# The inputs' part of an LSTM's gates: formed for eight steps at a time and turned by the identity, with the gates in three PSUM banks

## The chip, the core and the metric

The kernel runs on one core of a Trainium2 chip. The metric is the device time of one execution in microseconds; the time given is the median of several executions. The profile is one further execution, recorded by the hardware profiler; its span runs from the first to the last instruction on the core. Its engines are PE (matrix multiplication), DVE (vector), ACT (activation functions), POOL (general purpose) and SP (which here only issues DMA transfers).

## The reference

The inputs are `x`, 32 sequences of 512 rows with 256 features, and an adjacency matrix for each sequence. Two layers follow one another, each a graph attention and a sequence model, each with a layernorm ahead of it and the input added to what it gives. The last of the four parts is an LSTM with something behind it, and the change is about that:

```python
x_proj = jnp.einsum('btd,gd->btg', x, W_ih) + b_ih + b_hh
def step(carry, xp):
    h, c = carry
    gates = xp + h @ W_hh.T
    i, f, g, o = jnp.split(gates, 4, axis=-1)
    c = jax.nn.sigmoid(f) * c + jax.nn.sigmoid(i) * jnp.tanh(g)
    h = jax.nn.sigmoid(o) * jnp.tanh(c)
    return ((h, c), h)
...
logits = jnp.einsum('bth,lh->btl', lstm_out, W_lin) + b_lin
g = jax.lax.stop_gradient(jnp.argmax(logits, axis=-1)...)[..., None]
w = g * lstm_out
inc = jnp.cumsum(w, axis=1)
prefix = inc - w
suffix = inc[:, -1:, :] - inc
return 2.0 * lstm_out + prefix * fw_att + suffix * bw_att
```

Here B = 32 sequences, T = 512 steps, H = 256 hidden units, so 1024 gate values for each sequence and step. A step needs h of the step before: the 512 steps are a chain. The argmax over two logits is a comparison of their difference with a level. Everything is float32.

## The kernel before

The program has two stages. `layers_per_batch` does the first three parts sequence by sequence and leaves the result in DRAM as `X3`, with time outermost. `recurrence` then does the LSTM for all 32 sequences at once. Between the two stands a branch that is taken only for unusual data.

**Layout of a step.** The 256 hidden units are cut into Q = 4 groups of J = 64. Partition 32 q + b holds sequence b and group q, so the 128 partitions are full, and a gate of all sequences is 64 columns wide. The products therefore have 32 sequences as the stationary operand and run as four column tiles of 32 in PE, one for each q, each into its 32 partitions of PSUM. The launch code lays the gates down as i, f, o, g; `order` in `recurrence_weights` takes them as 1, 0, 3, 2, so a step has blocks of 64 columns for f, i, g and o, and two more columns for the difference of the logits and a zero. The sigmoid of v is taken as (tanh(v/2) + 1)/2, with the halves folded into the weights, so one tanh serves all gates. W = 258.

**A step in its parts.** PSUM has two tiles for a step, `pga` with 192 columns (f, i, g) and `pgb` with 66 (o, logit).
- `opened` (line 1201) starts each with the bias: a product of `one`, a row of ones in partition 0, with `bg`, which holds the biases in partition 0 and zeros elsewhere.
- `add_to` (line 1208) adds the inputs' part: the transposed input `xTr` of this step against `wih`, and later h against `whh`. Each is K = 256 deep, hence two products for each q.
- ACT takes the tanh of `pga` (line 1267) and of the o part of `pgb` (line 1268), into `z`, whose first 64 columns hold the cell.
- DVE forms `ab` (line 1270), (f+1)·c and (i+1)·g in one instruction over 128 columns, the new cell (line 1276), ACT its tanh `tc` (line 1278), DVE h as `hh` (line 1281) and its transpose within blocks of 32 (line 1283), which is what the next product needs.
- DVE then compares the logit that came with this step's product, which belongs to the step before (line 1289), and adds to the running sum `pp` (line 1293).

**Order.** The recurrence is written with the order of PE, DVE and ACT by hand: instructions stand in each engine's queue as the loop emits them. PE gets h's part of step t and then bias and inputs' part of step t+1, and in some steps the transposes of coming inputs. DVE gets behind the step one piece of `extra`: work for the chunk before or after. A chunk is CH = 16 steps. `normalised` loads four tiles `xt` of the next chunk (128 rows, 4 steps each), takes their statistics in steps 0 to 3, normalises them, and transposes them on PE in steps 11 to 14 (line 1142), ACT copying from PSUM (line 1145). `results` adds up the output of the chunk before in ten pieces (lines 1167 to 1179) and sends it to `R`, which stays in SBUF until the total over all steps is known; the last lines add that and write the output. DMA issues on SP are placed by the framework's scheduler.

**Weights.** `recurrence_weights` scales and reorders the weights on POOL during the layers and writes them to a DRAM tensor `wr`, and the biases to `wrb`; `recurrence` loads them with three DMAs from ACT (lines 1100 to 1102).

Of the kernel before, what the change touches and what calls it, by code (L numbers as in the profile page):

```python
# [19 lines left out]
P = 128  # L20
# [55 lines left out]
def layers_per_batch(ctx, tc, c, a, X3, odd=None, wr=None):  # L76
# [898 lines left out]
    if odd is not None:  # L975
        rw = ctx.enter_context(tc.tile_pool(name="rw0", bufs=1))
        parts = 2 + 2 + 2 * DK * 4
        streams.append(4.25 + nb / 2 * n / parts for n, _ in enumerate(recurrence_weights(nc, rw, a, wr)))
# [33 lines left out]
def recurrence_weights(nc, pool, a, wr):  # L1012
# [3 lines left out]

    Q, J = 4, 64
    W = 4 * J + 2
    nw = DK * Q * W
    order = ((1, 0.5), (0, 0.5), (3, 1.0), (2, 0.5))  # L1020
# [4 lines left out]
    def ordered(raw, n, s):  # L1025
        t = tile_(P, W, "rwt")
        nc.gpsimd.memset(t[:n, 4 * J :], 0.0)
        for to, (g, f) in enumerate(order):
            nc.gpsimd.tensor_scalar(t[:n, to * J : (to + 1) * J], raw[:n, g * J : (g + 1) * J], f * s, None, ALU.mult)
        return t  # L1030
# [3 lines left out]
    for q in range(Q):  # L1034
        for l in range(2):
            nc.sync.dma_start(
                out=wl[q * 32 : (q + 1) * 32, l * DK : (l + 1) * DK],
                in_=a.wl[q : q + 1, l * J : (l + 1) * J].rearrange("o (k p) -> p (o k)", p=32),
            )
    nc.gpsimd.tensor_tensor(wl[:, :DK], wl[:, DK:], wl[:, :DK], ALU.subtract)  # L1040
    yield
    bl = tile_(Q, 2, "rbl")
    nc.sync.dma_start(out=bl, in_=a.bl.to_broadcast([Q, 2]))
    b = [tile_(P, 4 * J, f"rwraw{n}") for n in range(2)]
    for t, src in zip(b, (a.bih, a.bhh)):
        nc.sync.dma_start(out=t[:Q], in_=src.rearrange("o (q r) -> (o q) r", q=Q))
    nc.gpsimd.tensor_tensor(b[0][:Q], b[0][:Q], b[1][:Q], ALU.add)
    t = ordered(b[0], Q, 1.0)
    nc.gpsimd.tensor_tensor(t[:Q, 4 * J : 4 * J + 1], bl[:, 1:2], bl[:, 0:1], ALU.subtract)
    nc.sync.dma_start(out=wr[1].rearrange("o (q w) -> (o q) w", q=Q), in_=t[:Q])  # L1050
    yield
    for n, src in enumerate((a.fw, a.bw)):
        t = tile_(P, W, "rwt")
        for q in range(Q):
            nc.sync.dma_start(out=t[q * GB : (q + 1) * GB, :J], in_=src[q : q + 1, :].to_broadcast([GB, J]))
        nc.gpsimd.tensor_scalar(t[:, :J], t[:, :J], 0.5, None, ALU.mult)
        nc.sync.dma_start(out=wr[0][:, 2 * nw + n * J : 2 * nw + (n + 1) * J], in_=t[:, :J])
        yield
    for n, (src, s) in enumerate(((a.wih, 1.0), (a.whh, 0.5))):
        for k in range(DK):  # L1060
            for q in range(Q):
# [8 lines left out]
                t = ordered(raw, P, s)  # L1070
                if n == 1:
                    nc.gpsimd.tensor_scalar(t[:, 4 * J : 4 * J + 1], wl[:, k : k + 1], 0.5, None, ALU.mult)
                o0 = n * nw + (k * Q + q) * W
                nc.sync.dma_start(out=wr[0][:, o0 : o0 + W], in_=t)
# [3 lines left out]
def recurrence(ctx, tc, c, a, X3, wr, out):  # L1078
# [6 lines left out]
    WA, WB = 3 * J, J + 2  # L1085
    W = WA + WB
# [5 lines left out]
    psg = ctx.enter_context(tc.tile_pool(name="psg", bufs=3, space=PSUM))  # L1092
    psx = ctx.enter_context(tc.tile_pool(name="psx", bufs=2, space=PSUM))


    wall = wp.tile([P, 2 * DK * Q * W + 2 * J], F32, name="wall")
    bg = wp.tile([P, Q, W], F32, name="bg")
    nc.gpsimd.memset(bg, 0.0)
    nw = DK * Q * W
    nc.scalar.dma_start(out=wall[:, :nw], in_=wr[0][:, :nw])  # L1100
    nc.scalar.dma_start(out=bg[0:1].rearrange("o q w -> o (q w)"), in_=wr[1])
    nc.scalar.dma_start(out=wall[:, nw:], in_=wr[0][:, nw:])
    wih, whh = (wall[:, n * nw : (n + 1) * nw].rearrange("p (k q w) -> p k q w", k=DK, q=Q) for n in range(2))
    fw, bw = (wall[:, 2 * nw + n * J : 2 * nw + (n + 1) * J] for n in range(2))
    one = wp.tile([P, GB], F32, name="one")
    nc.vector.memset(one, 0.0)
    nc.vector.memset(one[0:1, :], 1.0)
# [8 lines left out]
    def normalised(t0, out_):  # L1116
# [4 lines left out]
        for n in range(NX):  # L1121
            xt = xp_.tile([P, D], F32, tag=f"xt{n}", name=f"xt{t0}_{n}")
# [15 lines left out]
        def turn(n):  # L1138
# [4 lines left out]
            xT = xp_.tile([P, DK, P], F32, tag=f"xT{n}", name=f"xTr{t0}_{n}")  # L1143
            out_[n] = xT
# [4 lines left out]
    def results(t0, hh, gh, pp):  # L1149
# [9 lines left out]
        for s in (slice(0, n), slice(n, CH)):  # L1159
# [3 lines left out]
            m = gh[:, s, :]  # L1163
# [30 lines left out]
    PARTS = ((0, WA, "pga"), (WA, W, "pgb"))  # L1194

    def opened(t):

        pg = [psg.tile([P, e - s], F32, tag=tag, name=f"{tag}{t}") for s, e, tag in PARTS]
        for (s, e, _), p in zip(PARTS, pg):
            for q in range(Q):  # L1200
                nc.tensor.matmul(p[q * GB : (q + 1) * GB, :], one, bg[:, q, s:e], start=True, stop=False)  # L1201
        return pg

    def add_to(pg, x, w, stop):
        for (s, e, _), p in zip(PARTS, pg):
            for k in range(DK):
                for q in range(Q):
                    nc.tensor.matmul(  # L1208
                        p[q * GB : (q + 1) * GB, :], x[:, k, :], w[:, k, q, s:e],
                        start=False, stop=(stop and k == DK - 1),  # L1210
                    )

    def x_part(t, xT):

        pg = opened(t)
        r = (t % 4) * GB
        add_to(pg, xT[:, :, r : r + GB], wih, t == 0)
        return pg

    def blocks(z, n):  # L1220

        return bass.AP(tensor=z.tensor, offset=z.offset, ap=[list(z.ap[0]), [n * J, 2], [1, J]])

    with tc.manual_schedule(engines={mybir.EngineType.PE, mybir.EngineType.DVE, mybir.EngineType.Activation}):
        xT = [None] * NX
        stats, norms, turns = normalised(0, xT)
# [4 lines left out]
        nxt = [None] * NX  # L1231
        extra, turning = [], {}
        pg = x_part(0, xT[0])
# [4 lines left out]
        h = hh = gh = None  # L1238
        for t in range(T + 1):
            s = t % CH  # L1240
            last = t == T
            if s == 0 and not last:
                t0 = t
                hh_was, gh_was, pp_was = hh, gh, pp
                hh = ch.tile([P, CH, J], F32, tag="hh", name=f"hh{t0}")
                gh = ch.tile([P, CH, J], F32, tag="gh", name=f"gh{t0}")
                if t:
                    xT, nxt = nxt, [None] * NX
                    pp = ch.tile([P, CH + 1, J], F32, tag="pp", name=f"pp{t0}")
                assert not extra and not turning  # L1250
                stats, norms, turns = normalised(t0 + CH, nxt) if t0 + CH < T else ([], [], [])
                more = results(t0 - CH, hh_was, gh_was, pp_was) if t else []
                both = [lambda fs=norms[n : n + 2]: [f() for f in fs] for n in range(0, len(norms), 2)]
                extra = stats + more[:3] + both[:1] + more[3:4] + both[1:] + more[4:]
                turning = {CH - NX - 1 + n: f for n, f in enumerate(turns)}
            if last:

                pg = opened("last")
            if t:
                add_to(pg, h, whh, True)  # L1260
            pga, pgb = pg
            if not last:
                if t + 1 < T:
                    pg = x_part(t + 1, (xT if s + 1 < CH else nxt)[(s + 1) % CH // 4])
                turned = turning.pop(s)() if s in turning else None

                nc.scalar.activation(z[:, J : 4 * J], pga, AF.Tanh)  # L1267
                nc.scalar.activation(z[:, 4 * J :], pgb[:, :J], AF.Tanh)
                ab = st.tile([P, 2 * J], F32, tag="ab", name=f"ab{t}")
                nc.vector.scalar_tensor_tensor(  # L1270
                    ab.rearrange("p (a b) -> p a b", a=2), z[:, J : 3 * J].rearrange("p (a b) -> p a b", a=2),
                    1.0, blocks(z, 3), ALU.add, ALU.mult,
# [6 lines left out]
                if turned:  # L1279
                    turned()  # L1280
# [4 lines left out]
            if t:  # L1285

                i = (t - 1) % CH
                g_, p_, h_ = (gh_was, pp_was, hh_was) if s == 0 and not last else (gh, pp, hh)
                nc.vector.scalar_tensor_tensor(
                    g_[:, i, :], pgb[:, J : J + 1].to_broadcast([P, J]), 0.0, h_[:, i, :],  # L1290
# [122 lines left out]
```

## Time and profile before

| | before |
|---|---|
| median of 3 executions | 5133.64 us (5131.93 to 5137.21) |
| profiled execution, time | 5135.78 us |
| its span | 5134.1 us |
| layers, up to the first instruction of the recurrence | 3599 us |
| first tanh of a step to the last | 3613.0 to 5066.5 us |
| PE, DVE, ACT, POOL busy over the span | 83%, 64%, 55%, 21% |
| PE's granted clock, mean over the span | 0.936 |
| PE's granted clock, 500 to 3500 us, and 3700 to 5000 us | 0.93 to 0.94, and 1.00 |

Of the profile's views, four are used. The chain that ended last goes back from the last instruction to what released each one, and gives the shares of the span that lie on it by engine and line. The groups join instructions of the same line and tiles, with their number and mean duration in ns. The timeline gives instructions in order of time, neighbours of a kind merged, with their start and duration in us. The page of a line or tile gives durations as min/median/max and the times of the first and last one. In the last two, `128*32` is the size of the part of PE that an instruction uses and `x16` the number merged; a float32 product is two instructions. A PE duration includes the way through the array, so neighbours overlap; where one group follows another without a break, the time from start to start is what counts.

### The profile page before, as it was taken

The page shows a single profiled execution, that of the slowest core. Times are in us where ns is not written, and L with a number is a line of the kernel's source. Part 1 is how long each engine was busy: PE and PEld are TensorE (multiplying, and loading weights), DVE is VectorE, ACT ScalarE, POOL GpSimd, SP SyncE. Part 2 cuts the span into 40 slices and gives each one's busy share as a digit, 9 for nine tenths or more (in the row PEclk, how much of TensorE's full clock was granted, in tenths as well). Part 3 has the DMA queues.
Part 4 walks back from the last instruction along what each step waited for, and adds up shares of the span by engine and source line. Part 5 has one row for each costly group of instructions (what it writes and reads, how often), then busy time and mean ns, then how long its engine had stood idle before and what let it go on. Part 6 is the DMA issues. An engine that isn't in the chain of part 4 may idle for free. (4 is left out here: it accounts for less than half of the span.)

```text
span 5134.1 us, 129165 instructions
## 1 busy us (share of the span) xinstructions
PE 4260.7 (83%) x55022; PEld 2706.9 (53%) x55022; DVE 3279.2 (64%) x8158; ACT 2824.2 (55%) x5770; POOL 1096.5 (21%) x917
## 2 busy tenths in 40 slices
PE   4788888888888888888888888887788888888884
PEld 2344455444444445544445444454667666767663
DVE  3566666666666666666666666664566666666666
ACT  3677666776667766677666777664222222222221
POOL 4223232223332233322333223321000000000000
PEclk7899899999999999999999999998999999999997
DMA  3111112211122111211112121111211111111114
GB/s 107 56 60 54 56 55 69 65 50 60 50 66 66 56 58 52 66 63 60 58 52 66 58 64 58 52 42 33 61 41 34 37 39 41 41 37 37 38 36 150
DMA packets 272285, 288.48 MB, mean 56 GB/s; under 512 B 151509, under 2 KB 223025, under 8 KB 269522
## 3 DMA queue, kind: packets, MB, share of 16 engines
q1 hardware_dynamic: 268032, 268.09, 17.3%
q10 hardware_dynamic: 3506, 11.99, 0.7%
q8 instruction: 433, 7.09, 0.6%
q14 instruction: 154, 1.26, 0.1%
q0 software_dynamic: 160, 0.04, 0.0%
HBM read 226.04 MB, written 37.11 MB: 51 GB/s over the span
## 5 line engine op out<-in xcount | busy, mean ns | idle before, releaser
L1208 PE MATMUL pga<-wall,h 128*32 128x192 f32 x8176 | 438.3, 332 | 175.3 <-DVE h L1283 168.1
L1267 ACT ACTIVATE z<-pga 128x192 f32<-128x192 f32 x512 | 169.2, 330 | 691.8 <-PE pga L1208 684.5
L777 ACT ACTIVATE g<-bc,cs 128x128 f32<-128x128 f32 x1024 | 325.8, 390 | 341.1 <-PE py L803 334.8
L1208 PE MATMUL pga<-wall,xTr 128*32 128x192 f32 x8192 | 428.7, 326 | 0.0
L693 DVE SCALAR_TENSOR_TENSOR acc<-px,convw,acc 128x509 f32<-128x509 f32 (+2 forms) x480 | 341.6, 742 | 96.4 <-ACT acc L688 94.3
L533 PE MATMUL pav<-w,hb 128*64 128x512 f32 x1024 | 352.9, 617 | 60.2 <-DVE w L467 60.2
L461 ACT ACTIVATE w<-rb,neg,colsa 128x512 f32<-128x512 f32 x512 | 388.8, 804 | 8.0 <-DMA rb<-linea 4.3
L729 POOL TENSOR_TENSOR xdd<-xdt,dec 128x512 f32<-128x512 f32 x96 | 98.9, 1043 | 1348.9 <-DVE xdt L712 1348.4
L937 PE MATMUL pov<-wb,wv 128*128 128x257 f32 x1024 | 288.6, 450 | 106.7 <-DVE bnmv L66 94.9
L1208 PEld LDWEIGHTS pga<-wall,h 128*32 128x32 f32 x8176 | 213.6, 109 | 301.9 <-DVE h L1283 268.7
L803 PE MATMUL py<-g,xdt 128*64 128x128 f32 x2048 | 172.6, 320 | 225.9 <-DVE g L782 209.9
L467 DVE SCALAR_TENSOR_TENSOR w<-w,adjT 128x1024 f32<-128x1024 f32 x256 | 308.6, 1218 | 31.1 <-ACT w L461 31.1
L937 PEld LDWEIGHTS pov<-wb,wv 128*128 128x128 f32 x1024 | 232.8, 231 | 156.5 <-issue 113.0
L672 PE MATMUL px<-mT,win 128*128 128x512 f32 x640 | 300.6, 609 | 0.0
L54 POOL TENSOR_SCALAR ve<-mv 128x4 f32<-128x4 f32 x32 | 6.2, 193 | 1349.9 <-DVE mv L1129 1349.9
L1270 DVE SCALAR_TENSOR_TENSOR ab<-z 128x128 f32<-128x128 f32 x512 | 149.8, 293 | 224.0 <-ACT z L1267 224.0
L1278 ACT ACTIVATE tc<-z 128x64 f32<-128x64 f32 x512 | 131.4, 257 | 288.7 <-DVE z L1276 288.7
L790 POOL TENSOR_TENSOR xh<-xh,zs 128x512 f32<-128x512 f32 x128 | 179.6, 1404 | 512.1 <-DVE wb L926 348.5
L803 PEld LDWEIGHTS py<-g,xdt 128*64 128x64 f32 x2048 | 134.5, 160 | 280.8 <-DVE g L782 237.7
L822 PE MATMUL po<-wc,xh 128*128 128x256 f32 x1024 | 242.4, 391 | 27.6 <-POOL xh L790 27.4
L1201 PE MATMUL pga<-bg,one 128*32 128x192 f32 x4096 | 261.1, 326 | 0.0
L56 POOL TENSOR_TENSOR rs<-ve,mhalf 128x4 f32<-128x4 f32 (+1 forms) x192 | 255.0, 1328 | 16.0
(259 smaller groups left out, 9873.0 us busy)
## 6 DMA issues: line engine op xcount, KB each, us to landing
bc<-line SPq DMA_DIRECT2D x128, 512.0 KB
adj<-in_adj_dram SPq DMA_DIRECT2D x32, 1024.0 KB
rb<-linea SPq DMA_DIRECT2D x64, 512.0 KB
ce<-line SPq DMA_DIRECT2D x64, 384.0 KB
x<-in_x_dram SPq DMA_DIRECT2D x32, 512.0 KB
X<-x SPq DMA_DIRECT2D x32, 512.0 KB
xt<-X SPq DMA_DIRECT2D x128, 128.0 KB
x<-X SPq DMA_DIRECT2D x128, 128.0 KB
```

The lines of the kernel that those rows point to most:

```text
L56: nc.gpsimd.tensor_tensor(rs, ve, c.mhalf[:, :n], ALU.pow)
L461: nc.scalar.activation(w[:, t, k, :], rb[:, k, :], AF.Relu, bias=neg1, scale=cols[:, 2 * m + t, h + k : h + k + 1],)
L467: nc.vector.scalar_tensor_tensor(w[:, :, k, :], w[:, :, k, :], 1.0, edges, ALU.add, ALU.mult)
L533: nc.tensor.matmul(pa[k * HO : (k + 1) * HO, :], hb[:, j, 2 * q + k, :], w[:, t, k, :], start=(j == 0), stop=(j == NT - 1),)
L672: nc.tensor.matmul(pz, win[:, k, col : col + P], mT[:, k, :], start=(k == 0), stop=(k == DK - 1))
L693: nc.vector.scalar_tensor_tensor(acc[:, s:], pz[:, : N - s], convw[:, cc, k : k + 1], acc[:, s:], ALU.mult, ALU.add)
L777: nc.scalar.activation(g[:, i, k, :], bc[:, k, i * P : (i + 1) * P], AF.Relu, bias=cs[:, i, 2 * cc + k : 2 * cc + k + 1], scale=-1.0,)
L803: nc.tensor.matmul(py[k * HD : (k + 1) * HD, i * P : (i + 1) * P], xdt[:, i, h * HD : (h + 1) * HD], g[:, i, k, :], start=(i == 0), stop=F ...
L822: nc.tensor.matmul(po[:, i * D : (i + 1) * D], xh[:, cc, it * P : (it + 1) * P], wc[:, cc, :], start=(cc == 0), stop=(cc == NC - 1),)
L937: nc.tensor.matmul(po[:, : D + 1], ws[j // 2][:, j % 2, 0, it * P : (it + 1) * P], wb[:, j, :], start=(j == 0), stop=(j == NT - 1),)
L1201: nc.tensor.matmul(p[q * GB : (q + 1) * GB, :], one, bg[:, q, s:e], start=True, stop=False)
L1208: nc.tensor.matmul(p[q * GB : (q + 1) * GB, :], x[:, k, :], w[:, k, q, s:e], start=False, stop=(stop and k == DK - 1),)
```

## The change

The inputs' part is no longer formed step by step with the sequences as stationary operand. For a group of G = 8 steps the new function `units` forms it with the weights stationary: 128 gate units lie on the partitions, and the 8 steps times 32 sequences are 256 columns. There are eight such blocks of units for a group, and one block is formed in each step, for the group after the present one. ACT adds the bias as a column per partition (`bcol`) when it copies the block from PSUM (`pu`) to SBUF (`xu`). In a step, `x_part` takes the 32 columns of that step from `xu` as stationary operand and multiplies them by the identity (`turner`, with two zero columns), which turns them to the layout of a step and at the same time opens the PSUM tiles; `opened`, `bg` and `one` are gone.

The step's PSUM is three tiles: `pg0` (f, 64 columns, one buffer), `pg1` (i, g, 128 columns, two buffers) and `pg2` (o and the logit, 66 columns, two buffers). The pool of transposes `px` goes from two buffers to one, and `pu` has two. h's part is formed tile after tile, tanh is taken of each of the three, and `ab` is two instructions. The transposes of coming inputs move to steps 5, 6, 10 and 11, with the normalising ahead of the results' pieces; `xt` and `xTr` have one buffer each. The logit's bias is no longer in the product; the comparison is against a column `level`. The scratch for the results is a tile of its own, `m`, in place of the stored `gh`.

The weights' preparation has one more small write to `wr` for the level and one that spreads the biases to a column per partition; the inputs' weights lie in the order of units; its pieces are handed out in smaller portions. The three loads of `wall` go to SP, behind the loads of the first four `xt`.

```diff
@@ recurrence_weights
-    order = ((1, 0.5), (0, 0.5), (3, 1.0), (2, 0.5))
+    half = (0.5, 0.5, 0.5, 1.0)
+    for_x, for_h = (0, 3, 1, 2), (1, 0, 3, 2)
...
+    nc.sync.dma_start(out=wr[0][:, n0 + 2 * J + 8 : n0 + 2 * J + 9], in_=bl[:, 0:1])
+    nc.sync.dma_start(out=wr[1].rearrange("o (q w) -> (o q) w", q=Q), in_=t[:Q, : 4 * J])
+    yield
+    nc.sync.dma_start(out=wr[0][:, n0 + 2 * J : n0 + 2 * J + 8], in_=wr[1].rearrange("o (u p) -> p (o u)", p=P))
@@ recurrence
-    psg = ctx.enter_context(tc.tile_pool(name="psg", bufs=3, space=PSUM))
-    psx = ctx.enter_context(tc.tile_pool(name="psx", bufs=2, space=PSUM))
+    psg = ctx.enter_context(tc.tile_pool(name="psg", bufs=2, space=PSUM))
+    psx = ctx.enter_context(tc.tile_pool(name="psx", bufs=1, space=PSUM))
...
-    nc.scalar.dma_start(out=wall[:, :nw], in_=wr[0][:, :nw])
-    nc.scalar.dma_start(out=bg[0:1].rearrange("o q w -> o (q w)"), in_=wr[1])
-    nc.scalar.dma_start(out=wall[:, nw:], in_=wr[0][:, nw:])
...
+    turner = wp.tile([P, P + 2], F32, name="turner")
+    nc.vector.memset(turner[:, P:], 0.0)
+    nc.vector.tensor_copy(turner[:, :P], c.ident)
...
-    PARTS = ((0, WA, "pga"), (WA, W, "pgb"))
...
+    def units(t0, xT, out_, u):
+        if not u:
+            out_[t0] = xp_.tile([P, 2 * Q, G * GB], F32, tag="xu", name=f"xu{t0}")
+        xu = out_[t0]
+        pu = psx.tile([P, G * GB], F32, tag="pu", bufs=2, name=f"pu{t0}_{u}")
+        for k in range(DK):
+            nc.tensor.matmul(pu, wih[:, k, u, :], xT[:, k, :], start=(k == 0), stop=(k == DK - 1))
+        return lambda: nc.scalar.activation(xu[:, u, :], pu, AF.Identity, bias=bcol[:, u : u + 1])
+
+    PARTS = ((0, J), (J, 3 * J), (3 * J, W))
+
+    def x_part(t, xu):
+        pg = [
+            psg.tile([P, e - s], F32, tag=f"pg{n}", bufs=(1, 2, 2)[n], name=f"pg{n}_{t}") for n, (s, e) in enumerate(PARTS)
+        ]
+        r = (t % G) * GB
+        for p, half, (s, e) in zip(pg, (1, 0, 1), ((0, J), (0, P), (J, P + 2))):
             for q in range(Q):
-                nc.tensor.matmul(p[q * GB : (q + 1) * GB, :], one, bg[:, q, s:e], start=True, stop=False)
+                nc.tensor.matmul(
+                    p[q * GB : (q + 1) * GB, :], xu[:, 2 * q + half, r : r + GB], turner[:, s:e],
+                    start=True, stop=(t == 0),
+                )
         return pg
...
+        for s, e in ((0, nx), (n0, n0 + 2 * J + 9), (nx, n0)):
+            nc.sync.dma_start(out=wall[:, s:e], in_=wr[0][:, s:e])
...
+        for u in range(2 * Q):
+            units(0, nxt[0], xu, u)()
+        units(G, nxt[1], xu, 0)()
...
-                extra = stats + more[:3] + both[:1] + more[3:4] + both[1:] + more[4:]
-                turning = {CH - NX - 1 + n: f for n, f in enumerate(turns)}
+                extra = stats + both + more
+                turning = {(5, 6, 10, 11)[n]: f for n, f in enumerate(turns)}
             if last:
-                pg = opened("last")
-            if t:
-                add_to(pg, h, whh, True)
+                pg = [psg.tile([P, W - 3 * J], F32, tag="pg2", name="pglast")]
+                h_part(pg, h, PARTS[2:], True)
+            elif t:
+                h_part(pg, h)
...
-                    pg = x_part(t + 1, (xT if s + 1 < CH else nxt)[(s + 1) % CH // 4])
-                turned = turning.pop(s)() if s in turning else None
-                nc.scalar.activation(z[:, J : 4 * J], pga, AF.Tanh)
-                nc.scalar.activation(z[:, 4 * J :], pgb[:, :J], AF.Tanh)
+                    pg = x_part(t + 1, xu[(t + 1) // G * G])
+                g, u = divmod(t + 1, G)
+                g = (g + 1) * G
+                turned = [turning.pop(s)()] if s in turning else []
+                if g < T:
+                    turned.append(units(g, (xT if g < t0 + CH else nxt)[g // G % 2], xu, u))
+                for (s0, e0), p in zip(PARTS, pgs):
+                    e0 = min(e0, 4 * J)
+                    nc.scalar.activation(z[:, J + s0 : J + e0], p[:, : e0 - s0], AF.Tanh)
...
+                nc.vector.scalar_tensor_tensor(ab[:, :J], z[:, J : 2 * J], 1.0, z[:, :J], ALU.add, ALU.mult)
                 nc.vector.scalar_tensor_tensor(
-                    ab.rearrange("p (a b) -> p a b", a=2), z[:, J : 3 * J].rearrange("p (a b) -> p a b", a=2),
-                    1.0, blocks(z, 3), ALU.add, ALU.mult,
+                    ab[:, J:], z[:, 2 * J : 3 * J], 1.0, z[:, 3 * J : 4 * J], ALU.add, ALU.mult
                 )
...
-                    g_[:, i, :], pgb[:, J : J + 1].to_broadcast([P, J]), 0.0, h_[:, i, :],
+                    g_, pgs[-1][:, J : J + 1].to_broadcast([P, J]), level, h_[:, i, :], ALU.is_gt, ALU.mult,
```

## The prediction

> **What bounds the kernel now.** I read the chain that ended last first. It begins at 3599 us, where the recurrence begins, so the layers ahead of it are a block to be priced apart. In the chain DVE has 11% of the span, PE 9%, ACT 6%: a loop through three engines, none of them full.
>
> ```profile
> DVE 11%; PE 9%; ACT 6%; issue 3%; ACTq 0%; DMA 0%; DVEq 0%; SPq 0%
> ```
>
> Then the timeline of one step late in the loop (start, duration, engine, line, operation, tiles; in brackets the idle time before and what ended it).
>
> ```profile
> 4402.78 0.86 PE L1208 MATMUL pga<-wall,h 128*32 128x192 f32 x16 [0.43 <-DVE h L1283]
> ...
> 4403.45 0.41 PE L1208 MATMUL pgb<-wall,h 128*32 128x66 f32 x16
> ...
> 4403.68 0.51 PE L1201 MATMUL pga<-bg,one 128*32 128x192 f32 x8
> 4403.76 0.33 ACT L1267 ACTIVATE z<-pga 128x192 f32<-128x192 f32 x1 [1.58 <-PE pga L1208]
> ...
> 4403.99 0.22 ACT L1268 ACTIVATE z<-pgb 128x64 f32<-128x64 f32 x1
> ...
> 4404.12 0.84 PE L1208 MATMUL pga<-wall,xTr 128*32 128x192 f32 x16
> 4404.13 0.29 DVE L1270 SCALAR_TENSOR_TENSOR ab<-z 128x128 f32<-128x128 f32 x1 [0.43 <-ACT z L1267]
> 4404.45 0.22 DVE L1276 SCALAR_TENSOR_TENSOR z<-ab 128x64 f32<-128x64 f32 x1
> ...
> 4404.77 0.26 ACT L1278 ACTIVATE tc<-z 128x64 f32<-128x64 f32 x1 [0.56 <-DVE z L1276]
> 4404.77 0.42 PE L1208 MATMUL pgb<-wall,xTr 128*32 128x66 f32 x16
> 4405.06 0.23 DVE L1281 SCALAR_TENSOR_TENSOR hh<-z,tc 128x64 f32<-128x64 f32 x1 [0.38 <-ACT tc L1278]
> 4405.32 0.24 DVE L1283 STREAM_TRANSPOSE h<-hh 128x64 f32<-128x64 f32 x1
> ...
> 4405.62 0.86 PE L1208 MATMUL pga<-wall,h 128*32 128x192 f32 x16 [0.43 <-DVE h L1283]
> ```
>
> From start to start the loop is h's product to tanh 0.98, tanh to ab 0.37, ab to cell 0.32, cell to tc 0.32, tc to hh 0.29, hh to h 0.26, h to product 0.30: 2.84 us. The inputs' part runs beside it, and PE then idles 0.43 us for h. From the first h product (3614.80) to the last (5068.37) there are 511 periods in 1453.6 us, 2.845 each.
>
> Third, an early step and the answer on line 1267:
>
> ```profile
> 3617.52 0.86 PE L1208 MATMUL pga<-wall,h 128*32 128x192 f32 x16 [0.31 <-DVE h L1283]
> ...
> 3618.45 0.33 ACT L1267 ACTIVATE z<-pga 128x192 f32<-128x192 f32 x1 [1.51 <-PE pga L1208]
> ```
>
> ```profile
> L1267 ACTq EVENT_SEMAPHORE  x509: 17/17/17, 3621.2 to 5066.5; - x170
> ```
>
> Here the tanh stands 0.93 after its product, not 0.98; of 512 tanh, 509 have a second wait put ahead of them, from 3621.2 on. That wait costs 0.05 us on the path.
>
> **What the Trainium skill says.** "Perfetto Trace Analysis", Identifying Dependency Chains: an instruction that waits on several engines may get EventSemaphore instructions ahead of it. The trace agrees, with the 509 above. "TensorEngine Tiling (Array Packing)", Key Properties: changing the tiling mode drains TensorE. It agrees: in a step with transposes, pgb's last stream begins at 4427.49 and, at 0.23 us for such a row (4403.45 to 4403.68), ends at 4427.72; the 128*128 transpose starts at 4427.84, 0.12 later. "TensorE: Matmul & The Clock Gate", Architectural detail: PE can pull weight loads ahead of running matmuls. It agrees: eight 128*128 matmuls over 256 columns at L822 take 1.99 us, less the tail of a 379 ns one (1.99-0.38)/7 = 0.23 each, though each has a 190 ns load.
>
> **The change part by part.**
>
> *PE, h's part.* PE's time goes by columns: 16 rows of 192 take 0.67 us (4402.78 to 4403.45), 16 of 66 take 0.23. Split as 64, 128 and 66 it is 0.22+0.45+0.23, the same 0.90. i with g end where pga ended, f 0.45 earlier.
>
> *ACT.* The tanh of 192 becomes one of 64 (218 ns, as L1268) and one of 128. The latter has no row; it lies between 218 and 330, and the line through both gives 274. f's is ready at about 0.22 + 0.19 (rest of an 0.41 us group) + 0.12 to its start = 0.53 after the product, and ends at 0.75, before i and g need ACT at 0.93. In the built program f's tanh has the second wait, and that of i, g waits for PE alone. So the path loses 0.055 and 0.05. If the wait's cost doesn't follow, the latter is 0.
>
> *DVE.* ab of 128 (293 ns) becomes two of 64 (225, as L1276): 0.07 shorter, I take 0.065. f's half goes ahead, but behind the extra work of the step (0.69 us), which ends about 0.92 after the product; with independent work following at some 0.14 apart, i·g can start at about 1.1, and its input comes at 1.24. If that cover is gone the second half waits 0.1 or so. In the first step of a chunk the statistics end at 1.09, which still fits.
>
> Together 0.17 of 2.845: 511 x 0.17 = -86.9 us. The logits' comparison now takes a level from SBUF, 185 ns behind h, on nobody's path. The second pg2 buffer of before is gone: PE's x_part waits for the comparison two steps back, done by then. x_part also waits for f's tanh before it reopens the single pg0: 0.75 plus a release against 0.90, covered.
>
> *PE, inputs' part.* Removed: bias 0.45 (4403.68 to 4404.12 from its two rows) and x 0.90. Added: turning by the identity, 12 matmuls of 258 columns together, 0.45; and two matmuls of 256 columns in two passes each, 4 x 0.23 = 0.92. So PE's load stays about 2.25; it is the shape that changes: two changes of mode a step, 0.12 each. An ordinary step fills 0.90+0.45+0.12+0.92+0.12 = 2.51 of 2.675: hidden. A step with a transpose adds 0.28 (two 128*128 transposes, 0.44 less the tail of 0.16): 2.79, so the next product is 0.12 late. There are 31 x 4 = 124: between 0, if the last drain overlaps, and 0.15 each; I take 0.10: +12.4 us.
>
> *ACT, beside.* Each step gets one activation over 256 columns. The copy at L1145 takes 372 ns; "ScalarE: Activation LUTs", What ACT_TABLE_LOAD costs, prices a per-partition bias at 93 ns more: estimate 0.37 to 0.47. It starts when PE's units are out, about 2.6, ends at 3.05, which is 0.37 of the next step; f's tanh comes at 0.53. Hidden; what stands behind it on ACT is just that tanh.
>
> *Loads, buffers, layers.* xt in one buffer is loaded after its transpose of the chunk before (steps 5 to 11) and read from the next chunk's first step on, over 10 us later; on SP these loads stand between the x3 reads, also a chunk ahead. Work on the weights yields more often, but in the built program the order of the layers on PE, DVE and ACT is unchanged. SP gets two tiny transfers, one before adj, one before fw; the rb issue behind them waits until 50.76 anyway, and SP is free from 46.6. One memset less on POOL. 0 us, with 3 either way.
>
> *Start and end.* Before the first step eight unit groups and a ninth must be formed: 9 x 0.92, the first at the 0.5 clock that the windows from 3608 to 3612 show, some 9 us. Against this the first x part is 0.9 shorter, and the first loads, which took 5.6 us beside a 1 MB load of weights at up to 375 GB/s, go ahead of it on SP: 2 less. +6 us, between 3 and 9. The last product drops pga: -0.7.
>
> Sum: -86.9+12.4+6-0.7 = -69.2. The profiled execution took 5135.78 (span 5134.1 and 1.7 around it), so 5066.6; the median of the runs is 2.1 lower, 5133.64, so **5064**.
>
> **Rivals.** *PE becomes the bound* (0.18). The clock in the recurrence is 1.00, in the layers, full of 128*128 matmuls, 0.93. At 0.93 an ordinary step's h part costs 0.05 more (0.67/0.93), 2.725, and a transposing step 2.55/0.93+0.24 = 2.98: 387 x 2.725 + 124 x 2.98 = 1424, -29.6+5.3, time 5109. For: a third of PE's time becomes dense 128*128. Against: the load stays the same.
>
> *The split gains nothing* (0.06): f's half is late on DVE or ACT and the i, g tanh keeps its wait; only 0.055 remains, -28+18 = -10: 5123. Against: the slack worked out above.
>
> *Weight loads show* (0.08, slower). If the 190 ns loads aren't hidden with two tile modes in turn, each pass costs 0.42, PE's step is 2.51+0.76 = 3.27, and 511 x 0.43 = +217: 5351. It decides for the worse once a pass exceeds 0.23+0.33/4 = 0.31 us; then every step is bound by PE. L822 speaks against it.
>
> *Nothing moves* (0.03): the units arrive so late that ACT's queue takes back what is gained.
>
> **How the numbers follow.** The likeliest case has 0.65, with its own range from 5045 (no mode cost in transposing steps, a start of 3) to 5085 (0.15 there, 511 steps at 0.02 short of the gain). 8 in 10 needs the PE case up to about 5100, so 5043 to 5100. A gain or loss under 0.2% (10 us) is what can't be told from no change. Faster: 0.65+0.18 and most of the second rival, 0.88; same 0.04; slower 0.08.
>
> **What would show it.** Product to product 2.675 in ordinary steps and about 2.78 in those with a transpose; i·g's tanh 0.93 after the product and near 274 ns; a 225 ns second half on the path; PE still waiting for h in ordinary steps; the first tanh some 6 us later than 14.0 us after the recurrence's start; the layers' end at 3599. A clock under 1.00, or PE with no idle time before h, would make the prediction wrong upwards; units' passes over 0.31 us, its sign.

## The result, and the profile after

The changed kernel takes 5058.18 us (median of 4 executions, 5055.05 to 5059.54); the kernel before, measured beside it, 5135.14 us. The ratio is 0.985, with a 95% interval from 0.9833 to 0.9867. The forecast was 5064. The profiled execution took 5059.54 us with a span of 5057.8 us, 76.3 less than the span of before.

The chain that ended last, shares by engine, of the changed kernel:

```profile
PE 14%; DVE 9%; ACT 4%; issue 2%; DMA 0%; ACTq 0%; SPq 0%; DVEq 0%
```

DVE and ACT have lost on it (11% to 9% and 6% to 4%), PE has gained (9% to 14%). That looks like a kernel which PE now bounds, and the waits seem to say the same. Here are the waits of PE between 3700 and 4900 us (us in total, how often, the longest), of before:

```profile
PE pga L1208 <- DVE h L1283: 137.7, 318, 0.7
```

and of after:

```profile
PE pg L1241 <- DVE h L1316: 1.0, 3, 0.3
```

An experiment below shows that this reading is wrong for most steps. The timeline of an ordinary step of the changed kernel, late in the loop (start, duration, engine, line, operation, tiles; weight loads left out):

```profile
4409.43 1.10 PE L1241 MATMUL pg<-wall,h 128*32 128x64 f32 x48
...
4409.71 0.69 DVE L1182 TENSOR_TENSOR x<-x,hh 128x512 f32<-128x512 f32 x1
4409.98 0.22 ACT L1301 ACTIVATE z<-pg 128x64 f32<-128x64 f32 x1
4410.32 0.22 DVE L1303 SCALAR_TENSOR_TENSOR ab<-z 128x64 f32<-128x64 f32 x1
4410.34 0.63 PE L1231 MATMUL pg<-turner,xu 128*32 128x64 f32 x24
4410.36 0.45 ACT L1301 ACTIVATE z<-pg 128x128 f32<-128x128 f32 x2 [0.15 <-PE pg L1241]
4410.67 0.22 DVE L1304 SCALAR_TENSOR_TENSOR ab<-z 128x64 f32<-128x64 f32 x1
4410.90 1.13 PE L1217 MATMUL pu<-xTr,wall 128*128 128x256 f32 x4
4410.93 0.23 DVE L1309 SCALAR_TENSOR_TENSOR z<-ab 128x64 f32<-128x64 f32 x1
4411.25 0.26 ACT L1311 ACTIVATE tc<-z 128x64 f32<-128x64 f32 x1 [0.43 <-DVE z L1309]
4411.54 0.23 DVE L1314 SCALAR_TENSOR_TENSOR hh<-z,tc 128x64 f32<-128x64 f32 x1 [0.38 <-ACT tc L1311]
4411.80 0.25 DVE L1316 STREAM_TRANSPOSE h<-hh 128x64 f32<-128x64 f32 x1
...
4412.10 1.10 PE L1241 MATMUL pg<-wall,h 128*32 128x64 f32 x48
```

From start to start: product to the tanh of i and g 0.93 (0.98 before), that tanh to i·g's half of `ab` 0.31 (0.37), to the cell 0.26 (0.32), to `tc` 0.32, to `hh` 0.29, to `h` 0.26, to the next product 0.30: 2.67 in all, where the step of before had 2.84. The three gains of 0.05, 0.06 and 0.06 sit in the first three links, and f is early: its tanh at 0.55, its half of `ab` at 0.89, and DVE's extra work is out of the way in time for i·g at 1.24. The second wait of line 1301 has moved to f's tanh: in the answer on that line

```profile
L1301 ACT ACTIVATE z<-pg x1536: 217/224/284, 3618.2 to 4990.2; 128x64 f32<-128x64 f32 x128, 128x128 f32<-128x128 f32 x64
L1301 ACTq EVENT_SEMAPHORE  x509: 17/17/17, 3625.8 to 4989.5; - x170
```

there are 509 of them for 1536 tanh, one a step; in the step above it stands at 4409.92, right ahead of f's tanh.

A step with transposes, from the same timeline:

```profile
4406.72 1.10 PE L1241 MATMUL pg<-wall,h 128*32 128x64 f32 x48
...
4407.63 0.63 PE L1231 MATMUL pg<-turner,xu 128*32 128x64 f32 x24
...
4408.19 0.44 PE L1155 MATMUL pxt<-ident,xt 128*128 128x128 f32 x2
...
4408.47 1.03 PE L1217 MATMUL pu<-xTr,wall 128*128 128x256 f32 x4
...
4409.43 1.10 PE L1241 MATMUL pg<-wall,h 128*32 128x64 f32 x48
```

It takes 2.71. Its h was there at the usual place (`h` starts at 4409.09 and the product could follow 0.30 later, at 4409.39), so PE is late by 0.03 to 0.04.

**Where the time went.** Between the first and the last `h` lie 511 periods: 2.8446 us each before, 2.6844 after, which is -81.8 us. From the recurrence's first load of `xt` to the first `h` it took 15.49 us before (3599.02 to 3614.51) and takes 22.62 after (3597.07 to 3619.69): +7.1. The layers ended 1.95 us earlier. From the last `h` to the end 66.0 became 66.4. Together -76.3, the whole difference of the spans.

### The profile page after: what moved, and what is told of

The parts are those of the page before. It is cut to its first block, busy times and chain, and to the rows that moved or that the text cites. A ratio compares the mean times of both kernels' runs of the same rounds, so it can differ in the third digit from the quotient of the medians.

```text
span 5057.8 us, 126462 instructions
## 1 busy us (share of the span) xinstructions
PE 4323.2 (85%) x52926; PEld 2765.9 (55%) x52926; DVE 3340.9 (66%) x8670; ACT 3170.6 (63%) x6794; POOL 1099.1 (22%) x916
## 5 line engine op out<-in xcount | busy, mean ns | idle before, releaser
L1241 PEld LDWEIGHTS pg<-wall,h 128*32 128x32 f32 x24528 | 476.7, 109 | 229.2 <-DVE h L1316 227.8
L1241 PE MATMUL pg<-wall,h 128*32 128x64 f32 x24528 | 561.2, 239 | 35.0 <-DVE h L1316 10.3
L1217 PE MATMUL pu<-xTr,wall 128*128 128x256 f32 x2048 | 565.7, 399 | 0.0
L1301 ACT ACTIVATE z<-pg 128x64 f32<-128x64 f32 (+1 forms) x1536 | 346.9, 242 | 129.4 <-PE pg L1241 88.6
L1218 ACT ACTIVATE xu<-pu,wall 128x256 f32<-128x256 f32 x512 | 243.9, 476 | 277.9 <-PE pu L1217 276.5
L1217 PEld LDWEIGHTS pu<-xTr,wall 128*128 128x128 f32 x2048 | 348.9, 190 | 63.7
L1231 PE MATMUL pg<-turner,xu 128*32 128x64 f32 (+2 forms) x12288 | 323.4, 238 | 0.3 <-issue 0.2
L1231 PEld LDWEIGHTS pg<-turner,xu 128*32 128x32 f32 x12288 | 265.8, 110 | 1.9 <-issue 1.0
```

Of the source, the lines that this page charges most:

```text
L1217: nc.tensor.matmul(pu, wih[:, k, u, :], xT[:, k, :], start=(k == 0), stop=(k == DK - 1))
L1231: nc.tensor.matmul(p[q * GB : (q + 1) * GB, :], xu[:, 2 * q + half, r : r + GB], turner[:, s:e], start=True, stop=(t == 0),)
L1241: nc.tensor.matmul(p[q * GB : (q + 1) * GB, :], h[:, k, :], whh[:, k, q, s:e], start=(start and k == 0), stop=(k == DK - 1),)
L1301: nc.scalar.activation(z[:, J + s0 : J + e0], p[:, : e0 - s0], AF.Tanh)
```

## The experiments

**Theory.** The gain is that of the step's tail, cut in three: the second wait is off the path (0.05 us a step), the tanh ahead of the cell is shorter (0.055), and so is the half of `ab` behind it (0.065). Forming the inputs' part with units on partitions gives no time of its own; it costs about 7 us at the start and a little in the steps with transposes. **Rival:** the gain comes from taking the bias and inputs' products out of PE's column tiles. A second question was the idle time of PE that the profile no longer shows: is PE the bound?

**The split alone.** The kernel before, with three tiles, three tanh and two halves of `ab`:

```diff
-    PARTS = ((0, WA, "pga"), (WA, W, "pgb"))
+    PARTS = ((0, J, "pg0"), (J, 3 * J, "pg1"), (3 * J, W, "pg2"))
...
-                nc.scalar.activation(z[:, J : 4 * J], pga, AF.Tanh)
-                nc.scalar.activation(z[:, 4 * J :], pgb[:, :J], AF.Tanh)
+                for (s0, e0, _), p in zip(PARTS, pgs):
+                    e0 = min(e0, 4 * J)
+                    nc.scalar.activation(z[:, J + s0 : J + e0], p[:, : e0 - s0], AF.Tanh)
```

> The kernel before with the step's PSUM in three tiles (f; i with g; o with the logit), three tanh and ab in two halves; bias and inputs' part stay step by step in PE's column tiles as before. If the gain lies in the shorter way from h's product to the cell: i,g tanh 0.93 us after the product and about 276 ns, ordinary steps 2.67 us, the start as before; transposing steps at most 2.77; so 5135 - 511 x 0.17 = 5048, up to 10 more for the transposing steps: 5048 to 5058. Rival, the gain comes from taking bias and inputs' products out of PE's column tiles: steps stay at 2.84, time about 5135.

It took 5444.48 us, a ratio of 1.0599 (1.0572 to 1.0625): slower by 6%, which neither had expected. The mean step is 3.45 us. These are the lines in which its PE stood still, from one stretch of PE's timeline; "issue" means that nothing which the profile shows was being waited for:

```profile
4408.21 1.02 PE L1210 MATMUL pg<-wall,xTr 128*32 128x64 f32 x42 [1.47 <-issue]
...
4411.68 0.91 PE L1210 MATMUL pg<-wall,xTr 128*32 128x64 f32 x34 [0.92 <-issue]
...
4415.15 0.69 PE L1210 MATMUL pg<-wall,xTr 128*32 128x128 f32 x23 [0.81 <-issue]
...
4418.62 0.64 PE L1210 MATMUL pg<-wall,xTr 128*32 128x128 f32 x19 [0.71 <-issue]
...
4422.37 0.43 PE L1210 MATMUL pg<-wall,xTr 128*32 128x66 f32 x13 [0.51 <-issue]
```

PE starts again at 4408.21, 4411.68, 4415.15 and 4418.62, exactly 3.47 us apart, and each time at a later point of the step. No buffer of the kernel has such a beat. What has it is the fetch of instructions. The table of DMA queues has this row before:

```profile
q8 instruction: 433, 7.09, 0.6%
```

and this one in the split kernel:

```profile
q8 instruction: 593, 9.72, 0.7%
```

(packets, MB, share). A packet is 16.4 KB, and the 160 more packets stand for the instructions that the split adds on PE: three tiles instead of two make 120 matmul instructions of 80 in a step (the expectations call each of them a product), with their weight loads 240 instead of 160, and 80 more in 512 steps are 40,960, or 160 blocks of 256. One such block moves 1.1 us after each new start. Over 400 us the intervals from stall to stall are nearly all 3.47, 3.75 or 4.02, seldom 4.29; the two longest come mostly where other transfers run (between 3700 and 5200 us the median of what these move is 186 KB in an interval of 4.02, nothing in one of 3.47). So PE gets 256 instructions in 3.47 us at best, 13.6 ns each, and this kernel wants 240 of them in 2.67.

The Trainium skill, "Runtime: NRT & Kernel Launch", Instruction fetch mechanics, has blocks of 16 KiB or 256 instructions, fetched while the block before is executed, which agrees; it calls the fetch hidden because instructions are dispatched more slowly than they arrive. Here it isn't hidden, and the measurement decides.

Three kernels test that reading.

**More instructions, the same columns.** The kernel before with its own two tiles, tanh and `ab`; only the products over 192 columns are cut into 64 and 128:

```diff
-        for (s, e, _), p in zip(PARTS, pg):
+        for s, e, o, p in ((0, J, 0, pg[0]), (J, WA, J, pg[0]), (WA, W, 0, pg[1])):
```

> The kernel before, with the same two tiles, tanh and ab, but each of h's and the inputs' products over the 192 columns of pga cut into one over 64 and one over 128. The columns that PE streams are the same; the products go from 80 to 112 a step, 160 to 224 instructions with their loads. Theory (instructions come in blocks of 256, one each 3.47 us, which is 13.6 ns each): with some 4 more that wait, 228 x 13.6 ns = 3.09 us a step, or some 5% more as in the full split: 5135 + 511 x 0.25 to 0.40 = 5260 to 5340. Rival (it is the three tiles and their buffers that hold the full split up, or PE's columns): about 5135, steps 2.84.

Measured: 5328.8 us, a ratio of 1.0361 (1.0338 to 1.0384), steps of 3.246 us. PE's waits between 3700 and 5200 us:

```profile
PE pga L1208 <- issue: 117.5, 182, 1.8
PE pgb L1208 <- issue: 57.6, 88, 1.6
PE pga L1208 <- DVE h L1283: 51.7, 134, 0.7
```

PE streams the same columns as before and still loses 0.40 us a step, waiting for instructions; its stalls, too, are mostly 3.47, 3.75 or 4.02 apart. The number of instructions alone does it.

**The split with the inputs' product left out.**

```diff
-        add_to(pg, xT[:, :, r : r + GB], wih, t == 0)
+        if t == 0:
+            add_to(pg, xT[:, :, r : r + GB], wih, True)
```

> The kernel before split in three tiles as in the earlier run, but with the inputs' product left out of every step but the first (bias and h's part remain; the transposes and copies of inputs are still made). A step then has 72 float32 products on PE, 144 instructions with their loads, where the full split has 120 and 240, the kernel before 80 and 160. Theory: the full split is held up because PE's instructions arrive in blocks of 256 (16 KB), one each 3.47 us, and its steps need nearly one block each; below that the split works: i,g tanh 0.93 after the product, every step 2.67, time 5135 - 511 x 0.17 = 5048 or a few less. Rival: the single buffer of the f tile, or three groups per step, holds PE back whatever the number of instructions: steps stay near 3.4, 5400 or more.

Measured: 5046.02 us, a ratio of 0.9836 (0.9817 to 0.9855); 475 of 511 steps take 2.67 or 2.68. With 144 instructions a step the three tiles and f's single bank hold nothing up, and the step is that of the changed kernel. This shows the theory's main point: the step of 2.67 is the split's. It needs no units on partitions.

**The split with the bias left out**, as a point between the two:

> The kernel before split in three tiles, with the bias product left out of every step (h's and the inputs' products remain): 96 products, 192 instructions with their loads. Theory: 196 x 13.6 ns = 2.66 us a step, just at the length of the step of the split, so 2.67 to 2.80: 5046 to 5115. Rival (three tiles of column-tiled products on PE are the trouble): well above 3 us, as in the full split.

Measured: 5104.18 us (0.9934, from 0.9914 to 0.9954). 305 of 511 steps take 2.66 to 2.68, most of the others longer, up to 3.63, and PE waits for instructions now and then. At 192 a step a block of 256 is used up in 256/192 x 2.67 = 3.56 us, barely more than the 3.47 of its fetch, so a fetch that is delayed shows.

So the form with units does have a part in the gain, but another than the rival says. In the changed kernel h's part has 48 matmul instructions, the turning 24 and the units 4, as the timeline's counts show; with their loads 152 a step, against 160 before, where the split by itself has 240. The units pay for the split in instructions, not in columns.

**One term at a time: `ab` joined again.** The changed kernel, with

```diff
-                nc.vector.scalar_tensor_tensor(ab[:, :J], z[:, J : 2 * J], 1.0, z[:, :J], ALU.add, ALU.mult)
                 nc.vector.scalar_tensor_tensor(
-                    ab[:, J:], z[:, 2 * J : 3 * J], 1.0, z[:, 3 * J : 4 * J], ALU.add, ALU.mult
+                    ab.rearrange("p (a b) -> p a b", a=2), z[:, J : 3 * J].rearrange("p (a b) -> p a b", a=2),
+                    1.0, blocks(z, 3), ALU.add, ALU.mult,
                 )
```

> The changed kernel with ab in one instruction over 128 columns again. Theory: this puts back 0.065 us on the path, ordinary steps 2.735 and transposing ones the same, time 5058 + 387 x 0.065 + 124 x 0.03 = 5087. Rival: the join also lets DVE fill the idle time better and nothing is lost: 5058.

Measured: 5089.79 us, 31.6 more than the changed kernel (ratio to before 0.9915, from 0.9898 to 0.9931). Nearly all steps take 2.73 to 2.75, a median of 2.74: +0.07. The steps with transposes take 2.74 too, so they have PE's 2.71 hidden. The shorter tanh has no run of its own: its 0.055 is read from the durations, 330 ns before and 278 after, and from the link to `ab`, 0.37 and 0.31.

**The waits.** `tc` also has a second wait, in both kernels; in the changed one 509 times in 512:

```profile
L1311 ACTq EVENT_SEMAPHORE  x509: 17/17/17, 3627.1 to 4990.8; - x170
```

It goes when `tc` has four buffers, probably because the tanh of f has then already waited for what it guards:

```diff
-                tc_ = st.tile([P, J], F32, tag="tc", name=f"tc{t}")
+                tc_ = st.tile([P, J], F32, tag="tc", bufs=4, name=f"tc{t}")
```

> The changed kernel with four buffers for tc instead of three, so that the cell's tanh waits for DVE alone; nothing else moves. If the second wait there costs 0.06 us: cell to tc 0.26, ordinary steps 2.61, transposing steps still bound by PE at about 2.70; 5058 - 387 x 0.06 = 5035, and 5027 if the transposing steps gain too. Against the kernel with the wait put back at i and g, about 0.05 us a step less. Rival, the wait is absorbed by ACT's own latency: 5058.

Measured: 5035.89 us, a ratio of 0.9804 (0.978 to 0.9827). Ordinary steps take 2.61 (382 at 2.61 or 2.62), those with transposes 2.70 to 2.71. The timeline has the link from the cell to its tanh at 0.25, where it was 0.32:

```profile
4401.85 0.22 DVE L1309 SCALAR_TENSOR_TENSOR z<-ab 128x64 f32<-128x64 f32 x1
4402.10 0.26 ACT L1311 ACTIVATE tc<-z 128x64 f32<-128x64 f32 x1 [0.37 <-DVE z L1309]
```

The same edit on the kernel before:

> The kernel before with four buffers for tc instead of three, so that the cell's tanh waits for DVE alone. If a second wait on the path costs 0.06 us: every step 2.79 instead of 2.845, since PE has 0.43 us idle, time 5135 - 511 x 0.055 = 5107. Rival, it costs nothing: 5135.

Measured: 5109.53 us, a ratio of 0.994 (0.992 to 0.996); the mean step goes from 2.8446 to 2.7837. The 0.061 us a step times 511 are the 31 us of the medians.

The wait before i and g's tanh put back, in a kernel where `tc` has none:

```diff
+                zig = st.tile([P, 2 * J], F32, tag="zig", bufs=2, name=f"zig{t}")
...
+                nc.scalar.activation(zig, pgs[1], AF.Tanh)
```

> The changed kernel, with the tanh of i and g in a tile of its own with two buffers, so that the second wait stands before this tanh again, and, as a consequence, no longer before the cell's tanh (tc). If a second wait costs 0.05 to 0.06 us wherever it stands on the path: product to tanh 0.98 instead of 0.93, cell to tc 0.26 instead of 0.32, a step of 2.66 to 2.67, time within 6 us of 5058. Rival, only the wait on i and g's tanh costs, that on tc is nothing: step 2.72, time 5084.

Measured: 5061.94 us (0.985, from 0.9827 to 0.9873). Its answers on the two lines:

```profile
L1301 ACTq EVENT_SEMAPHORE  x510: 17/17/17, 3626.5 to 4993.8; - x170
L1312 ACT ACTIVATE tc<-z x512: 256/256/258, 3622.0 to 4994.7; 128x64 f32<-128x64 f32 x171
```

and its step:

```profile
4407.36 1.10 PE L1241 MATMUL pg<-wall,h 128*32 128x64 f32 x48
...
4408.36 0.28 ACT L1301 ACTIVATE zig<-pg 128x128 f32<-128x128 f32 x1 [0.21 <-PE pg L1241]
```

Product to tanh is 1.00 here (0.99 in the next step), and the ordinary step 2.67. Beside the kernel with four buffers of `tc`, at 2.61, only this wait (and the tile that brings it) differs: 0.06 us for one second wait. The rival, that only one of the two waits costs, falls: they cost the same.

**Is PE the bound?** The changed kernel with a third product over a block of units:

```diff
+        if t0 > G or (t0 == G and u):
+            nc.tensor.matmul(pu, wih[:, 0, u, :], xT[:, 0, :], start=True, stop=True)
         for k in range(DK):
```

> The changed kernel with one more product over the 256 columns of a block of units in every step (its result is overwritten by the next), so two more passes of 0.215 us and no other work. The prediction had 2.51 us of PE's time in an ordinary step; with passes of 0.215 instead of 0.23 it is 2.45, so an ordinary step comes to 2.88 instead of 2.67 and one with transposes to 2.71 + 0.43 = 3.14: 5058 + 387 x 0.21 + 124 x 0.43 = 5193, between 5165 and 5215. Rival, PE is already the bound of every step: 511 x 0.43 = 220 more, 5278.

Measured: 5219.25 us (1.0157, from 1.0137 to 1.0177), just above the range given. PE's timeline, a step with transposes and an ordinary one:

```profile
4399.81 1.10 PE L1243 MATMUL pg<-wall,h 128*32 128x64 f32 x48
4400.72 0.63 PE L1233 MATMUL pg<-turner,xu 128*32 128x64 f32 x24
4401.28 0.44 PE L1155 MATMUL pxt<-ident,xt 128*128 128x128 f32 x2
4401.55 0.60 PE L1217 MATMUL pu<-xTr,wall 128*128 128x256 f32 x2
4401.98 1.03 PE L1219 MATMUL pu<-xTr,wall 128*128 128x256 f32 x4
4402.94 1.10 PE L1243 MATMUL pg<-wall,h 128*32 128x64 f32 x48
4403.86 0.63 PE L1233 MATMUL pg<-turner,xu 128*32 128x64 f32 x24
4404.41 0.70 PE L1217 MATMUL pu<-xTr,wall 128*128 128x256 f32 x2
4404.95 1.03 PE L1219 MATMUL pu<-xTr,wall 128*128 128x256 f32 x4
4405.91 0.86 PE L1243 MATMUL pg<-wall,h 128*32 128x64 f32 x31
```

Steps with transposes now take 3.14 (median), 0.43 more than the 2.71 of the changed kernel, where PE bounds them: so two passes cost 0.43, a pass 0.215. Ordinary steps take 2.96 to 2.97. Less the 0.43, PE needs 2.535 in an ordinary step of the changed kernel, and has 0.135 to spare of its 2.67. The four buffers of `tc` say the same from the other side: the ordinary step got shorter by 0.06 with PE's work unchanged. That the waits show no idle PE has two reasons. The ends of the products are modelled: four passes are drawn as 1.03 us where only 0.96 pass from their start to the next product, in a step that PE bounds. And in the ordinary step of the changed kernel shown above there are 0.07 between the drawn end of the units (4410.90 + 1.13) and the next product at 4412.10, a gap that the waits don't list. The starts do show the slack: from the units' first pass to the next product it is 1.20 there, and 1.50 - 0.43 = 1.07 in the ordinary step just shown, without the added passes.

The lines also show why the transposes cost so little. The first two passes of the units take 0.54 in the ordinary step (4404.41 to 4404.95) and 0.43 behind the transposes (4401.55 to 4401.98). The starts of the single instructions in the changed kernel say where that lies. The second pass of the units starts 0.320 after the first where the turning stands in front, and 0.218 after it behind the transposes; the later passes are 0.216 apart. Of the two transposes the first takes 0.165 and the second 0.109. So the first 128*128 instruction of a step takes longer, by 0.10 if it is a pass over 256 columns and by 0.056 if it is a transpose. Two transposes thus add 0.165 + 0.109 - 0.10 = 0.17, not 0.28. It doesn't need a change of tile mode: in the kernel before the same 0.320 follows the first pass of line 822 in 32 of the 33 places where PE begins there after a wait, with a 128*128 pass ahead of the wait.

**A version faster than both kernels.** With four buffers for `tc`, the order of the tiles was changed so that f, with 64 columns, is the last tanh ahead of the cell:

```diff
-        for p, (s, e) in zip(pg, parts):
+        for n in (1, 0, 2)[: len(parts)] if len(parts) > 1 else (0,):
+            p, (s, e) = pg[n], parts[n]
```

> The changed kernel with four buffers for tc and with h's part in the order i,g - f - o, so that the last tanh ahead of the cell is f's of 64 columns (224 ns) and not that of 128 (278 ns); the inputs' part is turned in the order i,g - o - f, since f's single bank comes free later. Theory: ordinary steps 2.61 - 0.055 = 2.56, transposing steps unchanged at 2.71 by PE: 5036 - 387 x 0.055 = 5015. Rival: f's bank comes free too late (tanh ends 1.2 us after the product) and PE is bound in every step: 2.65 or more, 5050.

The inputs' part is turned in the order i,g - o - f, and i·g's half of `ab` stands ahead of f's.

Measured: 5027.34 us (0.9792, from 0.9775 to 0.9808), between the theory and its rival. Ordinary steps take 2.58, not 2.56. Then the transposes one by one, with the statistics of a pair turned into its scale before the next pair's:

```diff
-                extra = stats + both + more
-                turning = {(5, 6, 10, 11)[n]: f for n, f in enumerate(turns)}
+                extra = stats[:2] + both[:1] + stats[2:] + both[1:] + more
+                turning = {3 + n: f for n, f in enumerate(turns)}
```

> As the one before, with the eight transposes of a chunk in eight steps (3 to 10), one each, instead of two in each of four; for this the statistics and normalising are done pair by pair. Theory: a step with one transpose needs 2.71 - 0.215 = 2.5 us of PE, so it hides and all steps take 2.56: 5036 - 511 x 0.055 - 124 x 0.09 = 4997. Rival: two changes of tile mode cost as much with one transpose as with two, so eight steps of a chunk are bound at about 2.65: 5015 + 124 x 0.09 x (2 x 0.06 - 0.15)/0.09, which is 5011 to 5025.

Measured: 5020.2 us, a ratio of 0.9778 (0.9761 to 0.9794) to the kernel before, 38 us below the changed kernel, and in the range of the rival. The eight steps with one transpose take 2.60, the others 2.58, on the mean 2.599 where the kernel with the transposes in pairs has 2.617; 511 times that difference are 9 us, and the layers of this one execution ended 4.7 us later (the recurrence starts at 3603.6, not 3598.9), which hides half of it. The steps with a transpose don't hide it, though the theory had expected that they would. The transpose's 0.165 comes ahead of the units, which then start without their 0.10: 2.535 + 0.06 = 2.60 as an estimate of what PE needs, which is what these steps take. The timeline shows why f last brings 0.03 and not 0.055:

```profile
4405.68 1.10 PE L1248 MATMUL pg<-wall,h 128*32 128x128 f32 x48
...
4406.45 0.62 ACT L1309 ACTIVATE z<-pg 128x128 f32<-128x128 f32 x3 [0.23 <-PE pg L1248]
...
4406.76 0.23 DVE L1311 SCALAR_TENSOR_TENSOR ab<-z 128x64 f32<-128x64 f32 x1
4406.91 0.22 DVE L1314 SCALAR_TENSOR_TENSOR ab<-z 128x64 f32<-128x64 f32 x1
```

The tanh of i and g carries the second wait now and starts 0.77 after the product; f's runs on ACT right behind it, and f's half of `ab` right behind i·g's, 1.23 after the product, where i·g's half stood at 1.24 to 1.25. By the single records the tanh of i and g ends at 4406.73 and f's at 4406.85; i·g's half of `ab` starts 0.03 after its tanh, f's 0.06 after its own. So DVE's queue seems to be the later of the two, by 0.03; no run tests it.

## Why the prediction was right

Its time was 5.8 us too high. By its own steps:

- **h's part, second wait, tanh, `ab`** (0.17 a step): right in each term. The wait costs 0.055 to 0.06 where 0.05 was taken, the tanh of 128 has a median of 278 ns where 274 was estimated, the join of `ab` costs 0.07 where 0.065 was taken. Ordinary steps take 2.67 against 2.675.
- **f is early enough**: right. Its tanh starts at 0.55 (0.53 estimated), and i·g at 1.24 is not held by DVE.
- **PE in an ordinary step**, 2.51: measured 2.535. Two errors nearly cancel, which is luck. The passes take 0.216, not 0.23 (-0.06), and those of line 822, from which the 0.23 was taken, do so too: eight of them that take 1.99 begin with one interval of 0.32 and go on at 0.216, and (1.99-0.38)/7 spread the long interval over all seven. The units have that long first interval in every ordinary step, and it wasn't counted (+0.10). The rest, h's part and the two drains, comes to 0.02 less than the sum had.
- **Steps with transposes**: the term that was mis-sized. PE needs 2.705 and not 2.79, because two transposes add 0.17 to an ordinary step, not 0.28. The transposes themselves take 0.27, as counted; but the units behind them start without the 0.10. These steps are 0.033 longer than the others and not 0.10: +4 us for 124 of them instead of +12.4. That is 8.3 us; all in all the span fell by 76.3 where the sum had 69.2.
- **Start**: +7.1 against +6. The 36 matmul instructions of the units take 9.58 us, as "some 9" had it, and the first load lands 2.8 us after its issue instead of 5.6.
- **Identity on ACT**: 476 ns, at the upper end of 0.37 to 0.47 and just past it. In most steps it ends 0.11 before f's tanh, in about a quarter 0.02 after its start, as in the step above; f's tanh starts at 0.55 to 0.56 either way, so it lies off the path, as argued. The comparison with a level takes 243 ns instead of 185, off the path too.
- **Layers and end**: -1.95, within the 3 either way; the end +0.4 against -0.7.
- **A sign that was given wrongly**: "PE still waiting for h in ordinary steps" and "PE with no idle time before h". The waits show no idle PE, and the time was nevertheless that of the forecast. Idle time of PE in the waits is not a measure of its slack here.
- **What was not seen**: the prediction counts PE's columns and never its instructions. It came out right because the change lowers them from 160 to 152 a step; on this point that is luck. By the same way of counting the split without the units was expected at 5048 to 5058, and takes 5444. Nor does it mention the second wait at the cell's tanh, which the change leaves as it was.

The rivals fall with this. PE kept its clock of 1.00 from 3700 us on, the split did gain, and the passes stay below the 0.31 at which loads would have decided: the four of a block start 0.32 and then 0.216 apart, 0.24 on the mean. Whether the longer first interval is a part of a weight load is open.

## What to carry to other kernels

Count the instructions of TensorE as well as their columns: here a stretch that issues more than 256 in 3.47 us, weight loads included, is bound by their fetch, and the sign is "issue" in the waits with starts at equal intervals. In a short dependent loop price each second wait on ACT's path at 0.06 us, and look whether one more buffer lets another instruction have waited for it already. Whether an engine is the bound is told by giving it a known piece of work more, rather than by its busy share.

## What was not expected of the hardware

- PE's instructions, in straight code of this kernel, came at 256 in 3.47 us at best; intervals of 3.75, 4.02 and 4.29 us appeared too, the two longest mostly where other transfers ran. 224 a step gave steps of 3.25 us, 240 gave 3.45. The packet of a block took about 1 us in the split kernel; what fills the rest of the 3.47 is open.
- The first 128*128 instruction behind column tiles of 32, and at line 822 of the kernel before behind a wait, takes longer than those that follow: 0.320 to the next start against 0.216 over 256 columns, 0.165 against 0.109 for a transpose. As it comes without a change of tile mode too, a drain isn't needed for it; whether it is a weight load that can't be pulled ahead wasn't tried.
- A second wait costs 17 ns as an instruction and 0.055 to 0.06 us on the path.
